# Four graph layers in one kernel: grouping and side-by-side order of the pattern stage

## The chip, the cores and the metric

The kernel runs on one core of one Trainium2 chip. The metric is the device time of the whole program in microseconds (us), the median of three runs: 3212.45 us before the change (3210.42 to 3214.26). A profiled execution of the same program has a span of 3199.7 us; all times inside the kernel are from that profile, counted from the start of its span.

The core has five engines that take their instructions from queues of their own: TensorE (PE, with its weight loads shown apart as PEld), VectorE (DVE), ScalarE (ACT), GpSimd (POOL) and SyncE (SP, which issues most of the transfers).

## The reference

For 16 graphs ("batches") of 1024 nodes with 128 features, four residual layers are computed, each followed by a layer norm: an attention layer over the neighbours, a three-level convolution over a thinned ("dilated") adjacency, a dense neighbour sum, and a degree-normalised neighbour sum. The change concerns only the second layer's thinning:

```python
def step(carry, n):
    row = jnp.take(carry, n, axis=0)
    nbi = row.astype(jnp.int32)
    num = jnp.sum(nbi)
    sf = jnp.where(num > T_DIL, (num + K_DIL - 1) // K_DIL, 1)
    rank = jnp.cumsum(nbi)
    rm = row & (rank % sf == 0)
    valid = (mask_b[n] != 0) & (num > 1)
    rm = jnp.where(valid, rm, False)
    keep = ~rm
    carry = carry.at[n].set(row & keep)
    carry = carry.at[:, n].set(carry[:, n] & keep)
    return (carry, None)
out, _ = jax.lax.scan(step, adj_bool, jnp.arange(N))
```

The nodes are visited in order. A node with at most ten neighbours loses all of them (if it has more than one); a node with more loses the one or two whose rank is a multiple of half its count. A removal also removes the edge from the other end, so it changes the counts of later nodes. What the later stages need is which edges are left.

## The kernel before

Almost all nodes lose everything, so few edges survive. The kernel finds in each batch the up to 128 nodes with many neighbours ("candidates", put in slots) and works out their kept edges in a 128 by 128 table. It also finds the "lone" nodes that keep only their own loop. The stages run one after another: `phase_att` (layer 1), `phase_pattern` (the thinning), `phase_conv` (the convolution on what is left), `phase_end` (the last two layers). The change lies within `phase_pattern`, about 1697 to 2083 us.

`phase_pattern` has three kinds of work, each written as a Python generator that gives up control (`yield`) after each step:

- `find(b)`, one batch, ten `yield` lines of which one is in a loop of two: load the batch's 1024 by 1024 mask (L754, 2 MB, into one of three buffers `m`); count degrees (L760, 64 matmuls of one column); three passes of `earlier` (L777, L781); put the candidates in slots (`slots`, L714 to L719, which ends in the one-hot table `oh`); their node numbers and adjacency rows (L804 to L817, with a gathering transfer L810); the mask times the one-hot table (`pg`, L823, the last use of the mask) and from it `base` (L831); the 128 by 128 rank table `RB` (L837 to L844); the rows' values `V` (L851 to L861).
- `settle(g)`, half of the batches at once (8). The order of removals makes the counts depend on each other; a fixed point is reached in `ROUNDS` = 5 rounds. A round is a chain: small DVE operations on 128 x 8 numbers (L883 to L894), three wide ones over 128 x 1024 (`e1`, `e2`, `rm`, L896 to L898), eight matmuls of one column that count the removals (`pn`, L901), and the copy to `gone` (L903) that the next round starts from. After the rounds a tail (L905 to L953) makes the table of kept edges, normalises it, turns it and stores it.
- `alone(b)`, one batch, after its settle: rank all neighbours of the candidates (`prank`, L964), mark the removed ones (`hit`, L972), find the nodes that are left alone, put them in slots and gather their rows (L976 to L990).

`rolling` advances these generators in turn, one step of each open one per pass. Its list is one queue: the next task is opened only if fewer than `depth` = 5 are open, the one opened last has done `lag` = 2 steps, and all that the task needs has ended. A task that can't be opened yet holds back everything behind it. The list is: finds 0 to 9, settle 0, find 10, alone 0, find 11, alone 1 and so on to find 15 and alone 5, then settle 1, then the other alones.

This order of emission is not the order of the engines' queues. The program's framework lists each engine's instructions by a planner at build time, which goes by the order of emission as priority and by its own estimates of when an operand is ready; on the chip each queue then runs in its listed order. So steps of one task can stand between those of another: in the profile operations of settle 0 (L883, at 1835.04 us) stand between those of the finds.

Buffers that the tasks share: three masks `m`; four single PSUM banks `ps_s` (counts, `pn`, slots) and two double ones `ps_b` (`pg`, the turned rows, `prank`, and the settle's `py`, `pk`, `pt`); one buffer for each wide table of a settle (pool `lp`).

Of the kernel before, what the change touches and what calls it, by code (L numbers as in the profile page):

```python
# [10 lines left out]
F32 = mybir.dt.float32  # L11
# [6 lines left out]
ALU = mybir.AluOpType  # L18
# [4 lines left out]
B, N, F = 16, 1024, 128  # L23
P = 128
# [8 lines left out]
ROUND = 12582912.0  # L33
# [67 lines left out]
EDGE = 256.0  # L101
# [512 lines left out]

KEEP = 10
ROUNDS = 5
HALF = B // 2


# [12 lines left out]
    arrays["q_one_up"] = np.ascontiguousarray(np.broadcast_to(node[:P], (P, P)))  # L632


def rolling(tasks, depth, lag):


    todo, active, ended = list(tasks), [], set()
    while todo or active:
        while (  # L640
            todo and len(active) < depth and (not active or active[-1][2] >= lag)
            and all(n in ended for n in todo[0][2])
        ):
            active.append([todo[0][0], todo[0][1], 0])
            todo.pop(0)
        for a in list(active):
            try:
                next(a[1])
                a[2] += 1
            except StopIteration:  # L650
                active.remove(a)
                ended.add(a[0])
# [3 lines left out]
def phase_pattern(ctx, tc, t, c, mask_d, slots_d, x1_d, keep, flags):  # L656
# [5 lines left out]
    nc = tc.nc  # L662
# [4 lines left out]
    sm = ctx.enter_context(tc.tile_pool(name="q_s", bufs=4))  # L667
    lp = ctx.enter_context(tc.tile_pool(name="q_l", bufs=1))
    ps_s = ctx.enter_context(tc.tile_pool(name="q_ps", bufs=4, space=PSUM))
    ps_b = ctx.enter_context(tc.tile_pool(name="q_pb", bufs=2, space=PSUM))  # L670

    def load(name, shape, dtype=F16):
        w = kp.tile(shape, dtype, name=name)
        nc.sync.dma_start(w, t[name])
        return w
# [3 lines left out]
    same = load("q_same", [P, P])  # L679
# [17 lines left out]
    num0 = cp.tile([P, B], F32, name="num0")  # L697
    early = cp.tile([P, B], F32, name="early")
    v1 = cp.tile([P, B], F32, name="v1")
# [35 lines left out]
    def inner(k0, k1):  # L735

        k = slice(k0, k1)
        at = sm.tile([P, HALF], F32, name="at")
        none = sm.tile([P, HALF], F32, name="none")
        nc.vector.tensor_scalar(at, keep.node[:, k], -1.0, 0.0, op0=ALU.add, op1=ALU.max)  # L740
        nc.vector.tensor_scalar(none, keep.node[:, k], 0.0, float(N), op0=ALU.is_equal, op1=ALU.mult)
        nc.vector.tensor_copy(keep.inner[:, k], at)
        nc.vector.tensor_tensor(keep.row[:, k], at, none, ALU.add)
# [119 lines left out]

    def settle(g):

        bs = slice(g * HALF, (g + 1) * HALF)
        shape = [P, HALF, P]

        def tiny(name):
            return sm.tile([P, HALF], F32, name=name, bufs=3)  # L870

        def wide(name, dtype=F16):
            return lp.tile(shape, dtype, name=name)

        def spread(x):
            return x.unsqueeze(2).to_broadcast(shape)

        gone = tiny("gone")
        nc.vector.memset(gone, 0.0)
        rb = RB[:, bs, :]  # L880
        for k in range(ROUNDS):
            num, h, big, top = tiny("num"), tiny("h"), tiny("big"), tiny("top")
            nc.vector.scalar_tensor_tensor(num, num0[:, bs], 1.0, gone, op0=ALU.add, op1=ALU.subtract)  # L883

            nc.vector.tensor_scalar(h, num, 0.5, 0.25, op0=ALU.mult, op1=ALU.add)
            nc.vector.tensor_scalar(h, h, ROUND, None, op0=ALU.add)
            nc.vector.tensor_scalar(h, h, ROUND, None, op0=ALU.subtract)
            nc.vector.tensor_scalar(big, num, float(KEEP), None, op0=ALU.is_gt)


            nc.vector.scalar_tensor_tensor(v1[:, bs], h, EDGE - 1, gone, op0=ALU.add, op1=ALU.add)
            nc.vector.tensor_tensor(top, v1[:, bs], h, ALU.add)
            nc.vector.scalar_tensor_tensor(top, top, -EDGE, big, op0=ALU.add, op1=ALU.mult)
            nc.vector.tensor_scalar(v2[:, bs], top, EDGE, None, op0=ALU.add)  # L894
            e1, e2, rm = wide("e1"), wide("e2"), wide("rm")
            nc.vector.tensor_tensor(e1, rb, spread(v1[:, bs]), ALU.is_equal)  # L896
            nc.vector.tensor_tensor(e2, rb, spread(v2[:, bs]), ALU.is_ge)
            nc.vector.tensor_tensor(rm, e1, e2, ALU.max)  # L898
            pn = ps_s.tile([P, HALF], F32, name="pn", tag="ps")
            for j in range(HALF):  # L900
                nc.tensor.matmul(pn[:, j : j + 1], rm[:, j, :], one, start=True, stop=True)  # L901
            before, gone = gone, tiny("gone")
            nc.vector.tensor_copy(gone, pn)  # L903
            yield
        nc.vector.tensor_tensor(seen_moves[:, bs], gone, before, ALU.not_equal)  # L905
        nc.vector.tensor_scalar(below[:, bs], v2[:, bs], -0.5, None, op0=ALU.add)
        inner(g * HALF, (g + 1) * HALF)

        up = wide("up")
        nc.vector.scalar_tensor_tensor(up, rb, EDGE, rm, op0=ALU.is_ge, op1=ALU.is_gt)  # L910
        w1, w2 = tiny("w1"), tiny("w2")
        nc.vector.tensor_scalar(w1, h, EDGE, None, op0=ALU.add)
        nc.vector.scalar_tensor_tensor(w2, h, 2.0, big, op0=ALU.mult, op1=ALU.mult)
        nc.vector.tensor_scalar(w2, w2, EDGE, None, op0=ALU.add)
        py = ps_b.tile(shape, F32, name="py", tag="pb")
        for j in range(HALF):
            nc.tensor.matmul(py[:, j, :], up[:, j, :], run[:, :P], start=True, stop=True)
        y1, y2, low = wide("e1"), wide("e2"), wide("low")
        nc.vector.tensor_tensor(y1, py, spread(w1), ALU.not_equal)
        nc.vector.tensor_tensor(y2, py, spread(w2), ALU.is_lt)  # L920
        nc.vector.scalar_tensor_tensor(low, py, EDGE, y1, op0=ALU.is_ge, op1=ALU.mult)
        nc.vector.tensor_tensor(low, low, y2, ALU.mult)
        yield

        rank, k1, k2 = tiny("rank"), tiny("k1"), tiny("k2")
        nc.vector.tensor_tensor(rank, early[:, bs], gone, ALU.subtract)
        nc.vector.tensor_scalar(rank, rank, 1.0, None, op0=ALU.add)
        nc.vector.tensor_tensor(k1, rank, h, ALU.not_equal)
        nc.vector.scalar_tensor_tensor(k2, h, 2.0, rank, op0=ALU.mult, op1=ALU.not_equal)
        nc.vector.tensor_tensor(k1, k1, k2, ALU.mult)  # L930
        nc.vector.tensor_tensor(k1, k1, big, ALU.mult)
        nc.vector.scalar_tensor_tensor(k1, num, 1.0, k1, op0=ALU.is_le, op1=ALU.max)
        own = wide("own")
        nc.vector.tensor_tensor(own, same.unsqueeze(1).to_broadcast(shape), spread(k1), ALU.mult)
        pk = ps_b.tile(shape, F32, name="pk", tag="pb")
        for j in range(HALF):
            nc.tensor.matmul(pk[:, j, :], same, low[:, j, :], start=True, stop=False)
            nc.tensor.matmul(pk[:, j, :], same, own[:, j, :], start=False, stop=False)
            nc.tensor.matmul(pk[:, j, :], low[:, j, :], same, start=False, stop=True)
        yield  # L940

        d = wide("d", F32)
        nc.vector.tensor_tensor(d, V[:, bs, :], pk, ALU.mult)
        total = tiny("total")
        nc.vector.tensor_reduce(total, d, AX.X, ALU.add)
        nc.vector.tensor_scalar(total, total, 1.0, None, op0=ALU.max)
        nc.vector.reciprocal(total, total)
        nc.vector.tensor_tensor(d, d, spread(total), ALU.mult)
        pt = ps_b.tile(shape, F32, name="pt", tag="pb")
        for j in range(HALF):  # L950
            nc.tensor.transpose(pt[:, j, :], d[:, j, :], c.ident)
        nc.scalar.copy(d, pt)
        nc.sync.dma_start(slots_d[:, bs, :], d)  # L953
        yield
# [38 lines left out]
        )  # L993
        yield

    tasks = [(f"f{b}", find(b), []) for b in range(HALF + 2)]
    tasks.append(("s0", settle(0), [f"f{b}" for b in range(HALF)]))
    for b in range(HALF - 2):
        tasks += [(f"f{HALF + 2 + b}", find(HALF + 2 + b), []), (f"a{b}", alone(b), ["s0"])]
    tasks.append(("s1", settle(1), [f"f{b}" for b in range(HALF, B)]))  # L1000
    tasks += [(f"a{b}", alone(b), ["s0"]) for b in (HALF - 2, HALF - 1)]
    tasks += [(f"a{b}", alone(b), ["s1"]) for b in range(HALF, B)]
    rolling(tasks, 5, 2)
    inner(B, B + HALF)
    inner(B + HALF, 2 * B)
    for k in range(B, 2 * B):
        rows_of_x1(k)
# [1206 lines left out]
```

## Time and profile before

| stretch, us | what runs | length | PE busy | DVE busy | granted PE clock |
|---|---|---|---|---|---|
| 1697 to 1858 | finds 0 to 9, start of settle 0 | 161 | 137.8 | 75.0 | 0.76 |
| 1858 to 1897 | settle 0, start of find 10 | 39 | 15.2 | 32.9 | 0.55 |
| 1897 to 1997 | finds 10 to 15, alones 0 to 5 | 100 | 89.3 | 57.6 | 0.89 |
| 1997 to 2043 | settle 1, parts of alones | 46 | 13.2 | 40.1 | 0.57 |
| 2043 to 2083 | the last alones | 40 | 26.8 | 26.3 | 0.80 |

How to read it: a row's busy times are sums over the instructions of one engine in that stretch, so 15.2 of 39 means that PE stood still for 24 us. The granted clock is the share of full speed that TensorE was given. In lists of waits a line reads "who waited <- for whom: us in total, times, longest"; in lists of rows in order of time the columns are start, duration, engine, line, operation, out<-in, shape, and in brackets the idle time before it with what ended it. Matmul rows are pipelined, so a row's length is longer than the pace at which they follow each other: the 64 one-column matmuls of L760 take 1.74 us together though each is shown with 164 ns.

### The profile page before, as it was taken

How to read it: one execution, taken by the hardware profiler on the slowest of the kernel's cores; microseconds unless marked ns; L12 is line 12 of the kernel's file. 1: busy time of each engine (PE TensorE's matmuls, PEld its weight loads, DVE VectorE, ACT ScalarE, POOL GpSimd, SP SyncE). 2: the span in 40 equal slices, each digit the busy share in tenths (PEclk: the TensorE clock that was granted, in tenths of full speed). 3: DMA queues.
4: the chain of work that ended last, by engine and by line, in shares of the span. 5: the costliest groups of instructions: out<-in, count | busy, mean ns of one | idle time of the engine just before them, and what ended most of it. 6: DMA issues, size and time to landing. Idle time of an engine off the chain costs nothing. (4 is left out here: it accounts for less than half of the span.)

```text
span 3199.7 us, 70693 instructions
## 1 busy us (share of the span) xinstructions
PE 2800.9 (88%) x25724; PEld 2487.4 (78%) x25724; DVE 2251.8 (70%) x8226; ACT 1778.9 (56%) x5608; POOL 1271.8 (40%) x1280
## 2 busy tenths in 40 slices
PE   6999999999999999999996968477786899999997
PEld 3877877778777877788886858266676899999997
DVE  5878878788788878788774466746555566666665
ACT  3867777777776777777772323145645233333342
POOL 5645555454545454453113423243423223333221
PEclk8999999999999999999996878688988899999999
DMA  6422332223322332222023532044444434444441
GB/s 179 116 66 79 85 99 79 65 79 99 92 63 80 94 99 75 69 78 72 21 92 115 188 108 93 16 161 143 149 171 151 161 130 156 174 159 168 158 146 30
DMA packets 162023, 348.62 MB, mean 109 GB/s; under 512 B 14708, under 2 KB 68230, under 8 KB 161536
## 3 DMA queue, kind: packets, MB, share of 16 engines
q1 hardware_dynamic: 149760, 311.37, 30.6%
q0 software_dynamic: 10752, 28.42, 3.1%
q10 hardware_dynamic: 1152, 4.19, 0.5%
q8 instruction: 206, 3.38, 0.4%
q14 instruction: 153, 1.25, 0.1%
HBM read 257.87 MB, written 87.03 MB: 108 GB/s over the span
## 5 line engine op out<-in xcount | busy, mean ns | idle before, releaser
L272 POOL TENSOR_SCALAR mask<-ld 104x1024 f16<-104x1024 f32 (+1 forms) x150 | 443.2, 2955 | 548.1 <-PE pw L354 236.1
L434 PE MATMUL pg<-parts,oh 104*128 104x384 f32 (+1 forms) x1760 | 539.0, 382 | 49.7 <-ACT hg L452 49.1
L465 PE MATMUL pa<-hg,we 128*104 128x129 f32 (+1 forms) x3520 | 569.4, 277 | 1.8
L446 DVE SCALAR_TENSOR_TENSOR junk<-pg,w_a 128x128 f32<-128x128 f32 x1600 | 405.2, 283 | 173.3 <-PE pg L439 170.1
L465 PEld LDWEIGHTS pa<-hg,we 128*104 128x104 f32 x3520 | 498.0, 175 | 32.8 <-ACT hg L452 19.6
L452 ACT ACTIVATE hg<-pg,hg 128x128 f32<-128x128 f32 x1600 | 509.8, 370 | 17.1
L439 PE MATMUL pg<-parts,oh 104*128 104x384 f32 (+1 forms) x1760 | 473.2, 343 | 0.0
L434 PEld LDWEIGHTS pg<-parts,oh 104*128 104x128 f32 x1760 | 282.2, 193 | 78.4 <-ACT hg L452 62.0
L439 PEld LDWEIGHTS pg<-parts,oh 104*128 104x128 f32 x1760 | 314.6, 193 | 0.0
L450 ACT ACTIVATE hg<-sc 128x2 f32<-128x2 f32 (+1 forms) x880 | 188.6, 216 | 168.6 <-DVE junk L446 163.2
L419 DVE TENSOR_TENSOR we<-k_id,ids 128x832 f32<-128x832 f16 (+1 forms) x240 | 228.5, 952 | 8.5 <-PE pa L465 4.7
L1343 POOL TENSOR_TENSOR rstd<-ve,mhalf 128x4 f32<-128x4 f32 x96 | 97.0, 1010 | 323.9 <-DVE ve L1342 323.8
L389 ACT CAST oh<-oh_b 104x1024 fp32r<-104x1024 bf16 (+1 forms) x240 | 221.3, 977 | 1.9 <-DVE oh_b L385 1.7
L291 PE MATMUL pw<-w_all,xT 128*104 128x512 f32 x320 | 185.6, 664 | 17.0 <-DMA xT<-in_xTp 8.3
L1347 DVE TENSOR_SCALAR x<-x,mv,rstd 128x128 f32<-128x128 f32 x256 | 104.7, 449 | 92.6 <-POOL rstd L1343 92.6
L385 DVE TENSOR_TENSOR oh_b<-pw,k_slot_edge 104x512 bf16<-104x512 f32 (+1 forms) x240 | 144.6, 635 | 9.6 <-PE pw L384 7.1
L357 ACT CAST qs<-pw 104x416 f16<-104x416 f32 (+1 forms) x240 | 114.4, 477 | 66.4 <-PE pw L354 62.7
L364 DVE SCALAR_TENSOR_TENSOR one_way<-qs,mask 104x1040 bf16<-104x1040 f16 (+9 forms) x160 | 150.4, 940 | 0.1
L500 POOL TENSOR_TENSOR own<-parts 104x128 f32<-104x128 f32 x160 | 96.9, 637 | 118.4 <-DVE x_rows L521 82.4
L1452 ACT ACTIVATE y<-x,shift,rstd 128x128 f32<-128x128 f32 x128 | 52.7, 482 | 162.9 <-POOL shift L1445 162.9
L378 ACT CAST oh_b<-pw 104x512 bf16<-104x512 f32 (+1 forms) x240 | 133.1, 556 | 13.6 <-PE pw L377 13.5
L336 DVE TENSOR_TENSOR g<-k_slot,off 105x1408 f16<-105x1408 f16 x80 | 131.9, 1649 | 11.5 <-ACT off L332 11.4
(356 smaller groups left out, 6662.0 us busy)
## 6 DMA issues: line engine op xcount, KB each, us to landing
ld<-in_adjT SPq DMA_DIRECT2D x135, 416.0 KB
m<-mask_d SPq DMA_DIRECT2D x16, 2048.0 KB
keep_adj<-in_adjT SPq DMA_DIRECT2D x8, 4096.0 KB
adj<-in_adjT SPq DMA_DIRECT2D x8, 4096.0 KB
mask_d<-mask SPq DMA_DIRECT2D x144, 208.0 KB
hT_d<-uT SPq DMA_DIRECT2D x48, 512.0 KB
h<-hT_d SPq DMA_DIRECT2D x48, 512.0 KB
hT<-hT_d SPq DMA_DIRECT2D x32, 512.0 KB
```

Of the source, the lines that this page charges most:

```text
L272: engine.tensor_scalar(mt[:n, s, :N], ld[:n], 0.0, None, op0=ALU.is_gt)
L291: nc.tensor.matmul(pw[:W], xT[:, s * W : (s + 1) * W], w_all, start=True, stop=False, skip_group_check=True)
L364: nc.vector.scalar_tensor_tensor(junk[:W, :nb, :], q[:W, at : at + nb, :W], EDGE, mt[:W, i, i * W : NP].rearrange("p (n w) -> p n w", w=W) ...
L385: nc.vector.tensor_tensor(o[:W, n0 : n0 + m, 1, :], pw[:W, :m, :], k_slot_edge[:W].unsqueeze(1).to_broadcast([W, m, C]), ALU.is_equal,)
L389: nc.scalar.copy(wide.ends[:W, n0 : n0 + m], o[:W, n0 : n0 + m])
L419: nc.vector.tensor_tensor(we[:, :n, :], k_id.unsqueeze(1).to_broadcast([P, n, W]), wide.ids[:, 2 * lo : 2 * hi].unsqueeze(2).to_broadcast( ...
L434: nc.tensor.matmul(flat[:, first : 3 * F], own, d.parts[i][:W, p, first:], start=p == 0, stop=False, skip_group_check=True,)
L439: nc.tensor.matmul(pg[:, 1::step, :], other, reversed_parts(d.parts[j][:W, p, :], step), start=False, stop=p == 1, skip_group_check=True,)
L446: nc.vector.scalar_tensor_tensor(junk, pg[:, 1 + e, :], 0.0, w_a2, op0=ALU.max, op1=ALU.mult, accum_out=d.sc[:, at + e : at + e + 1],)
L450: nc.scalar.activation(hg[:, u - lo, :ways, F], d.sc[:, at : at + ways], AF.Exp)
L452: nc.scalar.activation(hg[:, u - lo, e, :F], pg[:, 3 - 3 * e, :], AF.Copy, scale=hg[:, u - lo, e, F : F + 1])
L465: nc.tensor.matmul(PA[bank][:W, at : at + part.stop - part.start], we[:, 2 * (u - lo) + e, :], hg[:, u - lo, e, part], start=False, stop=T ...
```

## The change

The fixed point is worked out for three groups of batches, 6, 6 and 4, instead of two of 8, so that the first can start after six finds. `rolling` gets a list of kinds: up to four finds, one settle and two alones are open at the same time, each kind with its own lag of two steps, and every task that may be opened is opened, whatever stands before it in the list. The list itself is now all finds, and then each settle with its alones. So finds go on while a settle runs, and alones of one group run beside the next settle. The arithmetic of a round is shortened: the count is kept with a half added, the rounding constant stays in `h` until the rounds are over, and two of nine small operations fall away. The change's own description also speaks of masks loaded into early space; no line of the diff does that, and the mask pool `q_m` is the first of the stage before and after.

```diff
--- before.py
+++ after.py
@@ -614,6 +614,7 @@
 
 KEEP = 10
 ROUNDS = 5
+GROUPS = ((0, 6), (6, 12), (12, 16))
 HALF = B // 2
 
 
@@ -632,21 +633,22 @@
     arrays["q_one_up"] = np.ascontiguousarray(np.broadcast_to(node[:P], (P, P)))
 
 
-def rolling(tasks, depth, lag):
+def rolling(tasks, most, lag):
+
 
 
     todo, active, ended = list(tasks), [], set()
     while todo or active:
-        while (
-            todo and len(active) < depth and (not active or active[-1][2] >= lag)
-            and all(n in ended for n in todo[0][2])
-        ):
-            active.append([todo[0][0], todo[0][1], 0])
-            todo.pop(0)
+        for task in list(todo):
+            name, kind, steps, after = task
+            same = [a for a in active if a[1] == kind]
+            if len(same) < most[kind] and (not same or same[-1][3] >= lag) and ended.issuperset(after):
+                active.append([name, kind, steps, 0])
+                todo.remove(task)
         for a in list(active):
             try:
-                next(a[1])
-                a[2] += 1
+                next(a[2])
+                a[3] += 1
             except StopIteration:
                 active.remove(a)
                 ended.add(a[0])
@@ -735,8 +737,8 @@
     def inner(k0, k1):
 
         k = slice(k0, k1)
-        at = sm.tile([P, HALF], F32, name="at")
-        none = sm.tile([P, HALF], F32, name="none")
+        at = sm.tile([P, k1 - k0], F32, name="at")
+        none = sm.tile([P, k1 - k0], F32, name="none")
         nc.vector.tensor_scalar(at, keep.node[:, k], -1.0, 0.0, op0=ALU.add, op1=ALU.max)
         nc.vector.tensor_scalar(none, keep.node[:, k], 0.0, float(N), op0=ALU.is_equal, op1=ALU.mult)
         nc.vector.tensor_copy(keep.inner[:, k], at)
@@ -863,11 +865,12 @@
 
     def settle(g):
 
-        bs = slice(g * HALF, (g + 1) * HALF)
-        shape = [P, HALF, P]
+        b0, b1 = GROUPS[g]
+        bs, n = slice(b0, b1), b1 - b0
+        shape = [P, n, P]
 
         def tiny(name):
-            return sm.tile([P, HALF], F32, name=name, bufs=3)
+            return sm.tile([P, n], F32, name=name, bufs=3)
 
         def wide(name, dtype=F16):
             return lp.tile(shape, dtype, name=name)
@@ -880,31 +883,30 @@
         rb = RB[:, bs, :]
         for k in range(ROUNDS):
             num, h, big, top = tiny("num"), tiny("h"), tiny("big"), tiny("top")
-            nc.vector.scalar_tensor_tensor(num, num0[:, bs], 1.0, gone, op0=ALU.add, op1=ALU.subtract)
-
-            nc.vector.tensor_scalar(h, num, 0.5, 0.25, op0=ALU.mult, op1=ALU.add)
-            nc.vector.tensor_scalar(h, h, ROUND, None, op0=ALU.add)
-            nc.vector.tensor_scalar(h, h, ROUND, None, op0=ALU.subtract)
-            nc.vector.tensor_scalar(big, num, float(KEEP), None, op0=ALU.is_gt)
-
-
-            nc.vector.scalar_tensor_tensor(v1[:, bs], h, EDGE - 1, gone, op0=ALU.add, op1=ALU.add)
-            nc.vector.tensor_tensor(top, v1[:, bs], h, ALU.add)
+
+            nc.vector.scalar_tensor_tensor(num, num0[:, bs], 1.5, gone, op0=ALU.add, op1=ALU.subtract)
+            nc.vector.tensor_scalar(h, num, 0.5, ROUND, op0=ALU.mult, op1=ALU.add)
+            nc.vector.tensor_scalar(big, num, KEEP + 0.5, None, op0=ALU.is_gt)
+
+
+            nc.vector.scalar_tensor_tensor(v1[:, bs], h, EDGE - 1 - ROUND, gone, op0=ALU.add, op1=ALU.add)
+            nc.vector.scalar_tensor_tensor(top, h, -ROUND, v1[:, bs], op0=ALU.add, op1=ALU.add)
             nc.vector.scalar_tensor_tensor(top, top, -EDGE, big, op0=ALU.add, op1=ALU.mult)
             nc.vector.tensor_scalar(v2[:, bs], top, EDGE, None, op0=ALU.add)
             e1, e2, rm = wide("e1"), wide("e2"), wide("rm")
             nc.vector.tensor_tensor(e1, rb, spread(v1[:, bs]), ALU.is_equal)
             nc.vector.tensor_tensor(e2, rb, spread(v2[:, bs]), ALU.is_ge)
             nc.vector.tensor_tensor(rm, e1, e2, ALU.max)
-            pn = ps_s.tile([P, HALF], F32, name="pn", tag="ps")
-            for j in range(HALF):
+            pn = ps_s.tile([P, n], F32, name="pn", tag="ps")
+            for j in range(n):
                 nc.tensor.matmul(pn[:, j : j + 1], rm[:, j, :], one, start=True, stop=True)
             before, gone = gone, tiny("gone")
             nc.vector.tensor_copy(gone, pn)
             yield
         nc.vector.tensor_tensor(seen_moves[:, bs], gone, before, ALU.not_equal)
         nc.vector.tensor_scalar(below[:, bs], v2[:, bs], -0.5, None, op0=ALU.add)
-        inner(g * HALF, (g + 1) * HALF)
+        nc.vector.tensor_scalar(h, h, -ROUND, None, op0=ALU.add)
+        inner(b0, b1)
 
         up = wide("up")
         nc.vector.scalar_tensor_tensor(up, rb, EDGE, rm, op0=ALU.is_ge, op1=ALU.is_gt)
@@ -913,7 +915,7 @@
         nc.vector.scalar_tensor_tensor(w2, h, 2.0, big, op0=ALU.mult, op1=ALU.mult)
         nc.vector.tensor_scalar(w2, w2, EDGE, None, op0=ALU.add)
         py = ps_b.tile(shape, F32, name="py", tag="pb")
-        for j in range(HALF):
+        for j in range(n):
             nc.tensor.matmul(py[:, j, :], up[:, j, :], run[:, :P], start=True, stop=True)
         y1, y2, low = wide("e1"), wide("e2"), wide("low")
         nc.vector.tensor_tensor(y1, py, spread(w1), ALU.not_equal)
@@ -929,11 +931,11 @@
         nc.vector.scalar_tensor_tensor(k2, h, 2.0, rank, op0=ALU.mult, op1=ALU.not_equal)
         nc.vector.tensor_tensor(k1, k1, k2, ALU.mult)
         nc.vector.tensor_tensor(k1, k1, big, ALU.mult)
-        nc.vector.scalar_tensor_tensor(k1, num, 1.0, k1, op0=ALU.is_le, op1=ALU.max)
+        nc.vector.scalar_tensor_tensor(k1, num, 1.5, k1, op0=ALU.is_le, op1=ALU.max)
         own = wide("own")
         nc.vector.tensor_tensor(own, same.unsqueeze(1).to_broadcast(shape), spread(k1), ALU.mult)
         pk = ps_b.tile(shape, F32, name="pk", tag="pb")
-        for j in range(HALF):
+        for j in range(n):
             nc.tensor.matmul(pk[:, j, :], same, low[:, j, :], start=True, stop=False)
             nc.tensor.matmul(pk[:, j, :], same, own[:, j, :], start=False, stop=False)
             nc.tensor.matmul(pk[:, j, :], low[:, j, :], same, start=False, stop=True)
@@ -947,7 +949,7 @@
         nc.vector.reciprocal(total, total)
         nc.vector.tensor_tensor(d, d, spread(total), ALU.mult)
         pt = ps_b.tile(shape, F32, name="pt", tag="pb")
-        for j in range(HALF):
+        for j in range(n):
             nc.tensor.transpose(pt[:, j, :], d[:, j, :], c.ident)
         nc.scalar.copy(d, pt)
         nc.sync.dma_start(slots_d[:, bs, :], d)
@@ -993,14 +995,11 @@
         )
         yield
 
-    tasks = [(f"f{b}", find(b), []) for b in range(HALF + 2)]
-    tasks.append(("s0", settle(0), [f"f{b}" for b in range(HALF)]))
-    for b in range(HALF - 2):
-        tasks += [(f"f{HALF + 2 + b}", find(HALF + 2 + b), []), (f"a{b}", alone(b), ["s0"])]
-    tasks.append(("s1", settle(1), [f"f{b}" for b in range(HALF, B)]))
-    tasks += [(f"a{b}", alone(b), ["s0"]) for b in (HALF - 2, HALF - 1)]
-    tasks += [(f"a{b}", alone(b), ["s1"]) for b in range(HALF, B)]
-    rolling(tasks, 5, 2)
+    tasks = [(f"f{b}", "find", find(b), []) for b in range(B)]
+    for g, (b0, b1) in enumerate(GROUPS):
+        tasks.append((f"s{g}", "settle", settle(g), [f"f{b}" for b in range(b0, b1)]))
+        tasks += [(f"a{b}", "alone", alone(b), [f"s{g}"]) for b in range(b0, b1)]
+    rolling(tasks, {"find": 4, "settle": 1, "alone": 2}, 2)
     inner(B, B + HALF)
     inner(B + HALF, 2 * B)
     for k in range(B, 2 * B):
```

## Prediction, made before the change was measured

> **What bounds the kernel now.** I read the page's busy times first, then its slices, the chain that ended last, a table by stage, the waits of each stage, and last the rows in order of time. The page says that TensorE (PE) leads, and the 40 slices (80 us each) show where it does not:
>
> ```profile
> PE 2800.9 (88%) x25724; PEld 2487.4 (78%) x25724; DVE 2251.8 (70%) x8226; ACT 1778.9 (56%) x5608; POOL 1271.8 (40%) x1280
> PE   6999999999999999999996968477786899999997
> PEclk8999999999999999999996878688988899999999
> ```
>
> PE is at 9 nearly throughout; the hole, down to 4, is slices 22 to 27, 1680 to 2160 us: the pattern stage. The chain that ended last holds none of its instructions, so I argue from the stage's own table. Its windows are cut where the work changes: finds 0 to 9; first fixed point (settle 0); finds 10 to 15 with six lone searches (alones); settle 1; the other alones. Columns: length, then busy us of PE, weight loads, VectorE (DVE), ScalarE (ACT), GpSimd (POOL), then PE clock, DMA share, GB/s:
>
> ```profile
> 1697.00:1858.00 161.00, 137.76 (x2850) 135.00 (x2848) 74.96 (x195) 49.53 (x138) 66.50 (x117) 0.76 0.52 168
> 1858.00:1897.00 39.00, 15.15 (x274) 14.04 (x272) 32.86 (x88) 2.78 (x6) 3.56 (x8) 0.55 0.07 25
> 1897.00:1997.00 100.00, 89.27 (x1700) 81.00 (x1701) 57.55 (x144) 37.66 (x93) 29.82 (x41) 0.89 0.33 105
> 1997.00:2043.00 46.00, 13.23 (x147) 10.11 (x146) 40.10 (x114) 2.81 (x5) 10.31 (x11) 0.57 0.04 11
> 2043.00:2083.00 40.00, 26.81 (x256) 16.33 (x256) 26.33 (x68) 11.13 (x18) 10.15 (x11) 0.80 0.08 22
> ```
>
> The stage takes 386 us in two regimes. With finds PE is busy 138 of 161 and 89 of 100 us; in the settles DVE is busy 33 of 39 and 40 of 46 while PE idles 24 and 33. Over the stage PE works 282 us and DVE 232, so either alone would fit in some 300. The waits say what PE idles for, first in the first settle, then in the second:
>
> ```profile
> PE pn L901 <- DVE rm L898: 15.7, 4, 4.9
> ...
> PE pn L901 <- DVE rm L898: 20.8, 4, 6.2
> ```
>
> Each round is DVE work, eight tiny matmuls and back to DVE. Only a find in hand can fill PE there, and few are.
>
> **What the Trainium skill says.** "Perfetto Trace Analysis", Optimization Strategy: a kernel with several regimes can gain from interleaving them. The table has the two it needs. "TensorE: Matmul & The Clock Gate", Part 2, Step-by-step: weight loads may be pulled ahead, matmuls stay in program order. The trace agrees: GpSimd reads find 10's mask at 1862.0, but its degree matmuls, queued behind a waiting pn, start only after that pn:
>
> ```profile
> 1874.52 0.37 PE L901 MATMUL pn<-q_run,rm 128*128 128x1 f16 x8 [4.89 <-DVE rm L898]
> 1874.76 1.39 PE L760 MATMUL pu<-q_run,m 128*128 128x1 f16 x47
> ```
>
> The same page, Part 1: an array that was idle runs at half clock until it has been busy. The trace agrees: the clock is 0.55 and 0.57 in the settles, and the 64 matmuls of one pg took 6.47 us at 1716 and 3.73 us at 1751.
>
> **The change part by part.** *Arithmetic of a round.* Nine tiny operations become seven (h loses two; num and big take the half with them), and one is added after the rounds. From "gone" at 2010.02 the chain steps 0.2 us per dependent tiny operation; two fewer save 0.4 us of a round that takes 5.26 us (gone 2010.02 to 2020.54, two rounds).
>
> *Groups of 6, 6 and 4.* The wide operations shrink. No row has 768 columns, so I bound it: 1.22 us for 1024 (L896) and 0.64 for 512 (L385). I take 0.93 for six batches and 0.64 for four; rm (0.69 for 1024) I scale to 0.55 and 0.41. A round of six: 5.26 - 0.4 - 2 x 0.29 - 0.14 = 4.14; of four: 5.26 - 0.4 - 2 x 0.58 - 0.28 = 3.42. The tail after the last gone took 15.3 and 16.2 us, say 15.7; seven operations of 1.22 and one of 0.69 in it sum to 9.2, and PE's pk took 2.2. Six batches: 15.7 - 2.3 - 0.6 = 12.8; four: 15.7 - 4.6 - 1.1 = 10.0. So alone a settle of eight is 42.0 us, of six 33.5, of four 27.1. Three settles are 94.1 us where two were 84: **laid end to end, the groups cost 10 us.** They pay only by overlap and an earlier start.
>
> *Start of the first settle.* The base product (L831) marks a find's end: 1722.7 for find 0, 1798.3 for find 5, 1831.0 for find 7, 1852.6 for find 9. Settle 0 began at 1835.0, 4 us after find 7's; now it needs find 5's and may begin at 1802, 33 us earlier.
>
> *Finds beside settles and alones.* The old list held find 11 and later behind the first alone, so behind all of settle 0: finds run out at 1858. The new one keeps up to four finds, one settle and two alones open by kind. PE's pace for a find is (1852.6 - 1722.7) / 9 = 14.4 us alone and, from find 11 (1931.3) to 15 (1992.5), 15.3 us with an alone beside it. Finds 6 to 15 take 144 to 153 us after 1798.3. The two settles of six add PE work of 6 us each (pn 5 x 0.38, py 0.9, pk 1.7, pt 1.5): the last base comes at 1954 to 1963 if PE never waits for a round. It will sometimes: pn stands among the finds' matmuls, and what is queued behind it is their next step, for which DVE then waits. PE idled 57 of 85 us in the old settles; two of six, 67 us, would give 45 us so. From zero to 45 I take a quarter, 11 us, since three masks are in SBUF and the queue can hold find work ahead of each pn. Last base: about 1970, against 1992.5: **22 us gained.**
>
> *The end.* After the last base the old kernel needed 2083 - 1992.5 = 90 us: settle 1 of eight, and ten alones. Now it is the settle of four, 27 us, with alones of group 1 filling DVE's waits, which are short, so I add rather than overlap: ten alones at 3.7 us of DVE (hit 1.28, oh 1.24, eight small ones near 0.15) are 37, and 6 to fill and drain: 70 us. **20 us gained.**
>
> *Loads.* Three mask buffers before and after; the mask pool already stands first. A load waits for the pg of three finds earlier:
>
> ```profile
> SPq L754 <- PE pg L823: 76.5, 7, 28.0
> SPq L953 <- ACT d L952: 148.1, 2, 100.1
> ```
>
> Four finds open instead of five cost no load, since three buffers allow no more. The second line warns: the settle's store stands in the same queue, and mask loads behind it wait for the settle's end. With a settle in mid-stream that can delay a find; it belongs to the slower cases.
>
> Sum: 22 + 20 = 42 us. 3212.45 - 42 = **3170 us**, 1.3% faster. The stages before 1697 and after 2083 keep their work; I give them nothing.
>
> **The rivals.** *Settles in series:* every pn holds the finds for the whole of its wait, so 45 us of stalls instead of 11. The gain is 42 - 34 = 8 us: 3204. For it: pn's waits of 4.9 us were not filled even by find 10, which was ready. Against it: there was only that one find, and at 1857.2 the first round's pn, with three finds in hand, waited in a busy queue while rm was done at 1843.7; PE lost 5 us there.
>
> *Slower:* finds depend on the number open, not on PE. Twelve steps of the list carried five finds in 75.6 us (base 0 to 5); with four in the same 75.6 us a find costs 18.9. That is 4.5 us more on about fifteen, 67, less the 42: +25, **3237**. For it: PE waits for the gathered rows (9.0 us) and masks (5.4) of the first stage. Against it: PE idles only 23 of 161 us there.
>
> *More:* PE keeps its full clock, since it stays fed. Fast rows give a find 12.4 us (degrees 1.74, three passes of 0.95, pg 3.73, pv 1.9, pt 0.9, the rest 1.3). Ten finds are 124, six alones at 2.6 are 16, settles 12: last base at 1950, and the first five finds could save 13 more. Gain 42 + 13 + 20 = 75: 3137. For it: 0.89 clock with finds and alones mixed. Against it: 0.76 with finds alone, though PE was 86% busy.
>
> **How the numbers follow.** Forecast 0.52, series 0.20, slower 0.15, more 0.13. The time is the forecast's, 3170. The range begins at 3125, below the "more" case by the 12 us that stalls of zero would add, and ends at 3215, past the series case by the 10 us of the extra settle; most of the slower case is left out above and a sliver below. Faster than 3206: 0.52 + 0.13 + most of the series case, 0.79; within 0.2%: 0.07; slower: 0.14.
>
> **What would show it.** Right: no stretch of 20 us in the stage with PE under half busy before the finds end; the first gone before 1825 instead of 1857.6; last base near 1970; pn's waits for rm well under the old 36.6 us in the first two settles together; the last alone near 2041. Series: those waits at 45 us or more and bases over 17 us apart while a settle runs. Slower: bases 18 us or more apart already before settle 0, with waits for rows or masks over 30 us. The forecast is wrong in size if the alones do not fit beside settle 2 or if the clock moves from 0.76.

## The result and the profile after

The changed kernel takes 3182.92 us (median of four runs, 3177.85 to 3185.33) against 3213.36 us for the kernel before, measured beside it: ratio 0.9903, 95% interval 0.9886 to 0.9920, so about 30 us or 1% faster. The forecast was 3170. The same changed kernel was measured twice more, beside other runs of the kernel before: 0.9947 (0.9930 to 0.9965) and 0.9919 (0.9895 to 0.9943). So the gain is 17 to 31 us by these ratios, and a difference of 10 us between two kernels counts here only if they ran side by side.

The profiled executions differ by less, 3199.7 against 3182.2 us: the execution of the kernel before that was profiled took 3201.61 us, some 12 us less than the median beside which it is set here (3213.36), and the changed kernel's 3184.05, 1 us more than its median. In which stage those 13 us lie is not shown. What follows accounts for the 17.5 us by which the two profiles differ. The page of the changed kernel, its busy times and slices of 80 us:

```profile
PE 2809.6 (88%) x25724; PEld 2496.2 (78%) x25724; DVE 2255.5 (71%) x8292; ACT 1779.1 (56%) x5609; POOL 1269.3 (40%) x1280
PE   6999999999999999999996888587786999999997
PEclk9999999999999999999996877698998999999999
```

The hole of PE is shorter and has no 4 in it. But PE does the same 25724 matmuls in 8.7 us more than before. The table by stage of the changed kernel, cut at: finds 0 to 6; settle 0 beside finds; finds with alones; settle 1 beside both; settle 2; the last alones (columns as in the table of the kernel before: length, busy us of PE, weight loads, DVE, ACT, POOL, PE clock, DMA share, GB/s):

```profile
1694.00:1815.00 121.00, 102.83 (x2168) 100.39 (x2169) 54.05 (x151) 34.85 (x98) 51.64 (x88) 0.75 0.49 157
1815.00:1870.00 55.00, 41.20 (x891) 39.98 (x889) 37.11 (x107) 13.90 (x41) 14.76 (x27) 0.62 0.35 116
1870.00:1920.00 50.00, 49.89 (x890) 45.80 (x889) 35.41 (x85) 18.01 (x40) 22.80 (x34) 0.88 0.52 172
1920.00:1987.00 67.00, 56.17 (x889) 51.06 (x888) 52.01 (x152) 21.22 (x56) 14.64 (x19) 0.76 0.22 69
1987.00:2028.00 41.00, 20.07 (x202) 13.89 (x202) 33.27 (x124) 7.50 (x13) 13.96 (x13) 0.70 0.08 23
2028.00:2062.00 34.00, 20.96 (x192) 12.62 (x192) 22.48 (x58) 8.66 (x14) 4.88 (x6) 0.75 0.03 9
```

The first two settles no longer stop PE: it is busy 41 of 55 us in settle 0 (was 15 of 39) and 56 of 67 in settle 1 (was 13 of 46). The two regimes do lie over each other. What is left of the hole is settle 2. The stage lasts 368 us instead of 386; PE idles 77 us of it instead of 104.

The waits of PE in the changed kernel, in settle 0 (first two lines), in settle 1 and in settle 2 (last line):

```profile
PE pn L902 <- DVE rm L899: 5.9, 3, 2.9
PE pu L762 <- DMA m<-mask_d: 4.4, 1, 4.4
...
PE pn L902 <- DVE rm L899: 0.5, 1, 0.5
...
PE pn L902 <- DVE rm L899: 14.0, 4, 4.5
```

A round's wait has shrunk from 15.7 us in settle 0 to 5.9, and from 20.8 in settle 1 to 0.5. It remains where no find is left, in settle 2.

Two lengths carry the comparison from here on: the **finds' stretch**, from the first degree matmul to the start of the last `base`, and the **end**, from there to the last `keep_lone`. Before: 295.7 + 90.6 us. After: 291.7 + 76.1. The forecast had asked for 22 us from the first and 20 from the second; the profile shows 4.0 and 14.5. The profiles of the changed kernel's two later measurements have 307.4 + 77.2 and 287.4 + 76.2 us: the end is steady to about 1 us, the finds' stretch is not, so a difference of 10 us in it between two profiles is weak evidence.

### The profile page after: what moved, and what is told of

It reads as the page before. It is cut to its first block, busy times and chain, and to the rows that moved or that the text cites. A ratio compares the mean times of both kernels' runs of the same rounds, so it can differ in the third digit from the quotient of the medians.

```text
span 3182.2 us, 70763 instructions
## 1 busy us (share of the span) xinstructions
PE 2809.6 (88%) x25724; PEld 2496.2 (78%) x25724; DVE 2255.5 (71%) x8292; ACT 1779.1 (56%) x5609; POOL 1269.3 (40%) x1280
## 5 line engine op out<-in xcount | busy, mean ns | idle before, releaser
L336 DVE TENSOR_TENSOR g<-k_slot,off 105x1408 f16<-105x1408 f16 x80 | 132.2, 1653 | 12.6 <-ACT off L332 12.5
```

## The experiments

Each verdict is a ratio to the kernel before, measured side by side, since the runs of the kernel before spread over 20 to 24 us in one set and their median stood at 3212.91 us beside the first four experiments, 3224.14 beside the second four (made on another chip), 3210.59 beside the last four.

### One part at a time

**Arithmetic alone**: the old list, two groups of eight, the short round.

```diff
-GROUPS = ((0, 6), (6, 12), (12, 16))
+GROUPS = ((0, 8), (8, 16))
...
-    rolling(tasks, {"find": 4, "settle": 1, "alone": 2}, 2)
+    rolling(tasks, 5, 2)
```

> Only the shortened arithmetic of a round: two groups of eight and the old single list, so ten rounds with two small operations less each. My theory (the gain comes from settles running beside finds, the arithmetic is worth 0.4 us a round): 4 us off, about 3209 us where the kernel before has 3213. Rival (the chain of small operations is the main cost of the settles, and the side-by-side list adds little): 15 us or more off, 3198 or less.

3199.52 us, ratio 0.9960 (0.9949 to 0.9971): 13 us, not 4, and nearer to the rival's 15. The stage in its profile is 382.1 us, 4.2 us shorter than before, which is the forecast's size. But the execution profiled here took 3202.4 us, no less than the 3201.61 of the kernel before, so the two profiles can't show where the other 9 us of the medians lie. That the arithmetic is worth 4 us and not more is the profile's word alone.

**Groups of 6, 6, 4 on the old list**, with the arithmetic:

```diff
-    rolling(tasks, {"find": 4, "settle": 1, "alone": 2}, 2)
+    tasks = [(f"f{b}", find(b), []) for b in range(8)]
+    tasks.append(("s0", settle(0), [f"f{b}" for b in range(6)]))
...
+    rolling(tasks, 5, 2)
```

> Groups of 6, 6 and 4 and the short arithmetic, but the old single list with five tasks open; each settle stands in the list two finds after the finds it needs, alones between later finds, as before. My theory: without the new list the three settles stand nearly end to end, 94 us less 4 us of arithmetic already counted against 84, and only the shorter last settle helps; 3200 to 3215 us. Rival (the smaller groups and their earlier start are the gain, whatever the list): 3183 to 3190, as the full change.

3210.53 us, ratio 0.9996 (0.9982 to 1.0010). That is what was expected, and 11.0 us above the run with the arithmetic alone (12.5 by the stages of the two profiles, 394.6 against 382.1). The forecast's 10 us set three settles with the short round, 94.1, against two with the long one, 84; against two with the short round, 80, the same working gives 14. This list also puts the settles and alones in other places, so it doesn't measure the groups by themselves. What it does measure is the new list: the full change differs from this run in the list alone and has ratios of 0.9903 to 0.9947, 16 to 30 us less. The list by kinds carries the gain.

**The new list with two groups of eight**, and the arithmetic:

```diff
-GROUPS = ((0, 6), (6, 12), (12, 16))
+GROUPS = ((0, 8), (8, 16))
```

> The new list by kinds and the short arithmetic, but two groups of eight. My theory: settle 0 runs beside finds 8 to 15 and is nearly free, but the last settle of eight stands alone, 40 us where the one of four takes 27 us; so about 13 us above the full change, 3196 us. Rival (groups are the gain): 3205 or more. Rival (the list is all, groups cost their 10 us): 3175 or less.

3189.48 us, ratio 0.9940 (0.9919 to 0.9961): some 7 us less than the 3196 that was expected. The list by kinds gives 10 us beyond the arithmetic by the medians, and by the stages of the two profiles (372.4 against 382.1); the ratios differ by 6 us and their intervals overlap. The full change's three ratios (0.9903 to 0.9947) lie around this one, so what three groups add to the new list can't be told from nothing here. The profile shows two effects that nearly cancel: with groups of eight the finds' stretch is shorter, 279.4 us against 291.7, and the end longer, 93.0 against 76.1.

**Five finds open instead of four:**

```diff
-    rolling(tasks, {"find": 4, "settle": 1, "alone": 2}, 2)
+    rolling(tasks, {"find": 5, "settle": 1, "alone": 2}, 2)
```

> The full change with up to five finds open instead of four. My theory (three masks and TensorE set the pace of the finds, not the number open): within 5 us of the full change, 3178 to 3188. Rival (four open are too few, this is where the forecast lost 12 us): 3173 or less.

3197.06 us, ratio 0.9955 (0.9941 to 0.9968), no better than any of the three measurements of the full change, and further from them than the 5 us of the theory. More open finds do shorten the finds' stretch, as the rival had it, to 277.5 us from 291.7, but the end grows from 76.1 to 96.8:

```profile
1694.80:1972.30 277.50, 236.70 (x4738) 226.65 (x4738) 160.21 (x450) 85.06 (x229) 98.35 (x162) 0.78 0.41 136
1972.30:2069.10 96.80, 53.82 (x486) 34.06 (x486) 71.15 (x224) 18.81 (x33) 23.80 (x25) 0.71 0.08 21
```

The settles and alones that gave way stand at the end, so the whole is not faster.

### Where do added rounds go?

> The full change again, as the base that the other three of this call are read against. All theories: as measured before, 3183 us (3178 to 3185), 30 us below the kernel before.

3204.97 us against 3224.14, ratio 0.9947: the base of the next three.

**Ten rounds instead of five in settles 0 and 1** (five are enough; the added ones repeat the fixed point):

```diff
-        for k in range(ROUNDS):
+        for k in range(ROUNDS * 2 if g < 2 else ROUNDS):
```

> Ten rounds instead of five in the settles of groups 0 and 1, the ones beside finds; the fixed point is already reached, so the output is the same. Ten added rounds of about 4.1 us. My theory (a settle beside finds costs the stage about a quarter of its length, since PE has find work to do): 10 to 15 us above the full change, 3193 to 3198. Rival (settles in series: each pn holds the finds): 41 us above, 3224. Rival (wholly hidden): within 4 us, 3187 or less.

3245.43 us, ratio 1.0075 (1.0058 to 1.0093): 40 us above the base, 4.1 us for each of the ten rounds. That is the number of the rival that lays the rounds in series (41), where 10 to 15 was expected. The finds' stretch and the end, first of the base, then of this kernel, tell how:

```profile
1697.00:2004.40 307.40, 254.98 (x4830) 240.33 (x4830) 174.67 (x491) 88.22 (x234) 101.73 (x168) 0.74 0.39 126
2004.40:2081.60 77.20, 41.86 (x394) 27.02 (x394) 56.91 (x183) 15.83 (x26) 17.82 (x19) 0.71 0.06 16
```

```profile
1695.80:2013.60 317.80, 249.96 (x4759) 236.26 (x4760) 183.19 (x518) 85.23 (x228) 96.24 (x161) 0.74 0.37 119
2013.60:2121.20 107.60, 56.50 (x527) 38.03 (x525) 81.84 (x266) 18.86 (x33) 25.19 (x25) 0.71 0.07 19
```

The finds' stretch grew by 10 us only, though six of the ten added rounds end in it, some 25 us at 4.1 each: rounds beside finds do hide in good part. The end grew by 30: settle 1 still has four rounds to do when the finds run out, so its alones and settle 2 start later, where no find covers them. DVE's work in the end rose from 56.9 to 81.8 us.

**Ten rounds in settle 2 alone:**

```diff
+        for k in range(ROUNDS * 2 if g == 2 else ROUNDS):
```

> Ten rounds instead of five in the settle of group 2 alone, after the last find; the output is the same. My theory (that settle stands alone, its rounds of 3.4 us are added): 17 us above the full change, 3200. Rival (alones of group 1 fill the waits, so rounds are partly hidden there too): 5 us above, 3188.

3217.48 us, ratio 0.9978 (0.9969 to 0.9988): 12.5 us for five rounds, between the 17 of the theory and the 5 of the rival, and the end is 14 us longer (91.2). The rounds of the last settle lie on the path; alones seem to hide a part. The finds' stretch, which this edit does not touch, is 6 us shorter in this profile (301.2), a measure of the noise between profiles.

**A smaller last group**, 6, 7 and 3:

```diff
-GROUPS = ((0, 6), (6, 12), (12, 16))
+GROUPS = ((0, 6), (6, 13), (13, 16))
```

> Groups of 6, 7 and 3. My theory (what is settled beside finds is cheap, what is settled after them is dear): the last settle loses one batch, 0.36 us a round and 1.9 of its tail, 4 us, and the middle one gains as much at a quarter of the price, so 3 us below the full change, 3180. Rival (order of the queues decides more than the sizes): more than 8 us either way, 3175 or less or 3191 or more.

3215.38 us, ratio 0.9974 (0.9962 to 0.9986): 10 us above the base where 3 below was expected, as the rival had it (more than 8 either way). Settle 1 now waits for find 12, and the end is 103.7 us with 77.4 us of DVE work in it instead of 77.2 with 56.9; in return the finds' stretch is 284.2 instead of 307.4, so the stages of the two profiles differ by 3 us only. It isn't the size of the last group that sets the end, but how much of the chain before it is still undone when the finds run out.

Five finds, groups of eight and this one agree: what leaves the finds' stretch comes back in the end, and more. From the last four I formed another theory: VectorE and the serial chain of settles set the stage, and TensorE's pace no longer does. In all these kernels the end lasts 1.3 to 1.4 times the DVE work in it, which spoke for it. The last four runs put it to the test.

### Which engine's time is paid for?

> The full change again, as the base of the three runs beside it: a ratio to the kernel before between 0.990 and 0.995, the two that it has shown.

3187.28 us against 3210.59, ratio 0.9919: the base.

**One wide DVE operation of each find moved to ScalarE:**

```diff
-        nc.vector.scalar_tensor_tensor(late, cand, 2.0 * N, node_col, op0=ALU.mult, op1=ALU.add)
+        nc.vector.scalar_tensor_tensor(late, cand, -2.0 * N, half_up, op0=ALU.mult, op1=ALU.add)
...
-        nc.vector.tensor_tensor(stay, late.unsqueeze(2).to_broadcast([P, T, P]), row_b, ALU.is_gt)
-        nc.vector.tensor_tensor(base[:, b], pg, stay, ALU.mult)
+        for ti in range(T):
+            nc.scalar.activation(stay[:, ti, :], row, AF.Sign, bias=late[:, ti : ti + 1])
+        nc.vector.scalar_tensor_tensor(base[:, b], stay, 0.0, pg, op0=ALU.is_lt, op1=ALU.mult)
```

> The full change with one wide VectorE operation of each find (the comparison that gives stay, 1221 ns in the changed kernel) made by ScalarE instead, as eight activations of 390 ns; the multiply of base reads their sign. VectorE loses 16 x 1.22 = 19.5 us, ScalarE gains 50 us. Theory now (the stage is set by VectorE work, in the finds and in the serial chain of the settles): 12 to 25 us faster than the full change. Rival (TensorE's pace in the finds sets it, as the forecast had it): within 5 us of it.

3176.49 us, ratio 0.9889 (0.9865 to 0.9912): 10.8 us below the base, between what the two theories expected, and the fastest median of all kernels here. Its interval overlaps the base's. DVE's busy time in the stage fell by 20.1 us, ScalarE's rose by 37.6, the stage itself fell by 2.0 (361.6 against 363.6), so at most a small part of the 10.8 is shown to come from there.

**The same DVE operation made twice:**

```diff
+        nc.vector.tensor_tensor(stay, late.unsqueeze(2).to_broadcast([P, T, P]), row_b, ALU.is_gt)
         nc.vector.tensor_tensor(stay, late.unsqueeze(2).to_broadcast([P, T, P]), row_b, ALU.is_gt)
```

> The full change with the same VectorE operation made twice in each find, the second over the first: 19.5 us more VectorE work and nothing else. Theory now: 15 to 25 us slower than the full change. Rival (TensorE's pace): 0 to 5 us slower.

3193.37 us, ratio 0.9945 (0.9926 to 0.9965): 6.1 us above the base, where the theory wanted 15 to 25:

```profile
1695.50:1990.00 294.50, 248.58 (x4819) 234.10 (x4820) 192.45 (x505) 88.06 (x233) 103.26 (x167) 0.76 0.39 130
1990.00:2065.70 75.70, 40.62 (x408) 26.39 (x406) 57.76 (x184) 16.10 (x27) 20.56 (x21) 0.75 0.07 19
```

Against the base, whose lines stand below, 14.4 us more DVE work in the stage cost 6.6 us; in the finds' stretch 13.6 us more cost 7.1.

**The degree matmuls made twice:**

```diff
-        for ni in range(T):
+        for ni in list(range(T)) * 2:
             for ci in range(T):
                 nc.tensor.matmul(
```

> The full change with the 64 one-column matmuls of the degree made twice in each find, the second over the first: 16 x 64 more matmuls, 28.6 us more of TensorE by the row of the changed kernel, and nothing on VectorE. Theory now (VectorE and the serial chain): 0 to 10 us slower than the full change. Rival (TensorE's pace in the finds): 20 to 29 us slower.

3209.05 us, ratio 0.9990 (0.9978 to 1.0003): 21.8 us above the base, which takes nearly the whole gain back, and is the rival's number. The finds' stretch and the end, first of the base, then of this kernel:

```profile
1696.90:1984.30 287.40, 245.58 (x4821) 232.97 (x4822) 178.90 (x490) 88.15 (x233) 102.45 (x168) 0.76 0.41 134
1984.30:2060.50 76.20, 42.40 (x406) 27.52 (x404) 56.94 (x183) 16.07 (x27) 18.70 (x18) 0.73 0.06 17
```

```profile
1700.50:2015.40 314.90, 278.76 (x5845) 264.35 (x5846) 172.61 (x491) 88.39 (x233) 102.25 (x168) 0.74 0.37 123
2015.40:2090.50 75.10, 41.25 (x405) 26.36 (x403) 56.87 (x183) 16.10 (x27) 18.70 (x19) 0.75 0.06 17
```

PE's busy time rose by 33.2 us in the finds' stretch and the stretch by 27.5; the end did not move. PE's waits for masks did not grow (12.8 us, 12.3 in the base), so the cost does not come from masks that are held longer. So my second theory fell for the finds' stretch: **up to the last base PE's time is paid for at some 80% by these profiles, DVE's at about half.** By the medians it is 22 of 33 us and 6 of 14. The order of the two is clear, the shares are not: each rests on one profile, and the doubled matmuls also stand at the start of a find's own chain, the doubled DVE operation near its end. After the last base the picture of the chain of rounds and alones stands, though no run doubles an operation there alone but for the rounds: the end is as long as what is left to do in it.

## Why the prediction was right, and what was mis-sized

**Groups, laid end to end: 10 us,** or 14 when the short round stands on both sides. Measured 11.0 (second run against the first), with other places in the list besides. The widths were bounded well: an operation of 768 columns took 0.95 to 0.99 us (taken: 0.93), one of 512 0.69 (0.64). A round of settle 2 without other work took 3.6 and 3.5 us (gone at 2008.54, 2012.16 and 2015.66), forecast 3.42.

**Start of the first settle.** First gone at 1825.8 us, 0.8 us past the forecast's "before 1825", and 32 us before the old 1857.6.

**PE no longer waits for rounds.** The waits for rm in the first two settles are 6.4 us instead of 36.6. So the series rival is not how the unaltered change behaves. No 20 us before the last base have PE under half busy; the lowest are 11.9, in 1843 to 1863. It is these signs that count. The time alone would say little, since the range of 3125 to 3215 holds the series rival's 3204 too. One of that rival's signs did come: bases over 17 us apart while a settle runs, 29.3 and 27.2 us beside settle 0 (finds 7 to 9) and up to 19.6 beside settle 1. Finds do slow down beside a settle, but not by waits for its rounds. And two signs of the forecast did not come: the last base is at 1985.7, not near 1970, the last alone at 2061.8, not near 2041.

**The middle: 22 us forecast, 4.0 measured. This is the term that failed**, in the step "Finds 6 to 15 take 144 to 153 us after 1798.3", with 12 us for the settles' PE work and 11 for stalls: 167 to 176 us from base 5 to base 15. Here is that stretch, in the kernel before, in the changed one, and in its later profile:

```profile
1798.28:1992.55 194.27, 149.71 (x2846) 139.65 (x2843) 120.67 (x307) 59.32 (x151) 59.09 (x89) 0.81 0.37 119
```

```profile
1795.24:1985.65 190.41, 162.84 (x2879) 152.24 (x2880) 136.95 (x375) 59.45 (x153) 65.72 (x96) 0.75 0.36 117
```

```profile
1801.59:1984.31 182.72, 157.01 (x2879) 146.43 (x2880) 135.93 (x376) 59.61 (x153) 66.22 (x96) 0.80 0.37 122
```

By the later profile the finds' stretch gained 8.3 us instead of 4.0; the term is too large either way, unless most of the 13 us that the profiles leave open lie here. Idle time of PE: 44.6 us before, 27.6 and 25.7 after. The forecast's pace of 14.4 us a find, with PE 86% busy, holds some 20 us of idle time in ten finds, and with the 11 for stalls that makes 31: the idle time was sized nearly right. What was wrong is PE's own time. By the same working it is 136 to 144 us (86% of 144 to 153, and 12 for the settles); it was 149.7 already in the old kernel, so the pace of the first nine finds was too kind, and it is 162.8 and 157.0 in the changed one, for 33 more matmuls out of 2879. The clock moved: 0.81 before, 0.75 after, and 149.71 x 0.81 / 0.75 = 161.7, close to the 162.84 seen. The later profile's 0.80 gives 151.6 only, where 157.0 was seen, but the clock of a stretch is a mean that counts PE's idle time too. One group shows it better, with equal counts, `pg` in this stretch, before and after:

```profile
L823 PE MATMUL pg<-oh,m 128*128 128x128 f16 x640 | 40.3, 227 | 0.8 <-DVE oh L719 0.8
```

```profile
L825 PE MATMUL pg<-oh,m 128*128 128x128 f16 x640 | 49.3, 251 | 3.5 <-DVE keep_index L733 1.2 <-DVE oh L721 1.2 <-ACT turned L858 1.1
```

The same 640 matmuls took 9.0 us more of PE's time (47.6 us in the later profile, so 7.3 more). The records of the granted clock in the traces hold only two values, 0.5 and 1.0. Averaged over the time in which `pg` ran, the clock was 0.92 before, 0.76 after and 0.79 in the later profile, and busy time times this clock is 37.2, 37.3 and 37.5: the clock accounts for all that `pg` lost. It is no accident of the one profile of the kernel before: in the run with the arithmetic alone, on the old list, `pg` took 39.9 us and PE 151.2 in the same stretch. One-column matmuls did not lose: 512 of the degree took 14.4 us before and 14.2 after. So 17 to 19 us of idle time were won, as meant, and 7 to 13 us given back as longer PE time, most of it in `pg`.

Why the clock fell stays open; no run changes it alone. "TensorE: Matmul & The Clock Gate", Part 1, of the Trainium skill has a gate with two states, half and full clock, set by how busy the array was in windows of about 3.4 us. The traces agree on the two states; what sets them no run here shows. In the first profile the clock is lowest where finds and settle 0 share PE (0.62 at 41 of 55 us busy), which would fit: the old kernel had one long hole and then a long run at 0.89; the new one has short holes and is at half clock more of the time. The forecast named the clock as what could make it wrong in size, but had its rival on the other side only, at full clock.

**Loads: "Four finds open instead of five cost no load".** Not quite. PE's waits for masks in the stage went from 5.4 to 12.5 us. The queue of transfers, in the changed kernel:

```profile
SPq L756 <- PE pg L825: 88.5, 6, 32.0
SPq L955 <- ACT d L954: 101.8, 2, 61.3
```

The loads wait longer for `pg`, the last use of a mask (76.5 us before). Beside settle 0 no `pg` ended between find 7's (its base is at 1822.8) and find 8's (1852.1), so no mask came free in those 29 us, and the next degrees waited 4.4 us for theirs, until 1862.9. With five finds open PE's waits for masks are 12.2 us, so it is not the number of open finds. That it is the buffers is argued from this trace; a fourth mask buffer was not tried.

**The end: 20 us forecast, 14.5 measured.** The likeliest place of the 6 us is the first round of settle 2. In order of time in the changed kernel:

```profile
1992.19 0.42 DVE L899 TENSOR_TENSOR rm<-e,e 128x512 f16<-128x512 f16 x1
...
1994.46 2.00 PE L862 MATMUL pv<-oh,turned 128*128 128x128 f32 x16
1996.31 0.97 PE L966 MATMUL prank<-q_run,base 128*128 128x512 f16 x4
...
1998.27 1.68 PE L966 MATMUL prank<-q_run,base 128*128 128x384 f16 x10
...
2001.50 0.24 PE L902 MATMUL pn<-q_run,rm 128*128 128x1 f16 x4
2001.77 0.16 DVE L904 COPY gone<-pn 128x4 f32<-128x4 f32 x1
```

rm is done at 1992.6, but its four tiny matmuls start 8.9 us later: they stand in PE's queue behind `pv` of the last find and two alones' `prank`. PE is busy 8.7 of these 8.9 us; it is the place in the order that costs. The forecast added settle and alones without such a wait, though the old kernel shows a like one that the forecast names: rm done at 1843.7, its pn at 1857.2. No run takes this wait away, so that it is worth 6 us is not shown. The next round takes 6.8 us, with alones' DVE work inside it, the others 3.5 to 3.9.

**Arithmetic: 4 us in the working, left out of the sum as part of the round.** By the profile 4.2, by the medians 13 (see the first run).

**The sum**: 4.0 + 14.5 = 18.5 us of the stage by the profile, 30 by the medians of that measurement, 19 and 23 by the two later ones, where 42 was forecast. The direction and the mechanism were right, the time within the range, the gain too large in both terms; of the 17 to 19 us of idle time won in the middle, 7 to 13 went back as longer PE time.

## What to carry to other kernels

When two regimes are laid over each other, count the gain in idle time of the engine that is to be filled, and then check at which clock it will do its own work: a mixed stretch with short holes can be slower per matmul than a hole followed by a dense run (251 against 227 ns here). A chain that hides beside other work can still cost its full length, 40 us for ten added rounds here, if what depends on it is thereby pushed past the end of that work, so cost it at the end of the stage, not where it stands. An order that brings one kind of work forward leaves another for the end, so compare whole stages. And to learn which engine's time is paid for, make a harmless operation twice on each and compare: this separated two theories that the busy shares could not. Before two profiles are compared, see how far each profiled execution lies from its kernel's median.

## What the hardware showed that was not expected

A PE that the records call busy need not be at full clock. Two stretches of 20 us in the changed kernel:

```profile
1700.00:1720.00 20.00, 19.02 (x505) 18.38 (x505) 9.18 (x31) 4.00 (x13) 10.60 (x24) 0.59 0.12 35
1880.00:1900.00 20.00, 20.00 (x351) 18.65 (x349) 13.60 (x31) 11.63 (x29) 9.62 (x15) 1.00 0.87 289
```

In the first, PE is busy 19.0 of 20 us, mostly with one-column matmuls of the first finds, at 0.59; in the second, 20.0 of 20 us at 1.00. In the first the clock stayed at 0.50 up to 1716.5, though PE was busy 11.0 of the 12 us from 1700 to 1712, and stood at 1.00 for the rest of the stretch, 3 us after the first `pg` began (64 matmuls of 128 columns, from 1713.51). Whether one-column matmuls count for the clock no run here tests. And the clock is not the same from one profile to the next of one kernel: 0.75 and 0.80 from base 5 to base 15 of the changed kernel, 190.4 and 182.7 us. Nor is it from one execution to the next: of the 21 runs of the kernel before beside the last four experiments the shortest, 3204.79 us, has a mean clock of 0.923, the longest, 3228.81 us, 0.913.
